# Second token half of a Winograd-form gated feed-forward kernel: transposed on TensorE, or read transposed and scaled in place

## The chip, the cores and the metric

The kernel runs on one core of one Trainium2 chip. The time is the device time of one execution in microseconds (us), told as the median over runs. Five engines take part, each working through its own list of instructions in order: PE (TensorE, matrix products; PEld is its load of stationary operands), DVE (VectorE), ACT (ScalarE), POOL (GpSimd) and SP (SyncE, which here issues nearly all DMAs). An instruction that waits holds back everything behind it on its engine.

## The reference, cut to what matters

```python
x  = L0_attn_data                      # (2, 1024, 512): 2048 tokens, 512 features, float32
xn = (x - mean(x)) / sqrt(var(x) + 1e-5)             # per token
s  = xn @ (weight * block_mask).T                    # 512 -> 512
nx = xn * rsqrt(mean(xn**2) + 1e-5) * ln_w
g  = silu( (silu(nx @ gate_w.T) * (nx @ up_w.T)) @ down_w.T )   # 512 -> 1792 -> 512
out = x + s * g
```

All of it is float32. The kernel normalises a token with a factor `scl` and an offset `nb` (so `xn = x * scl + nb`), both from the token's mean and variance, and feeds the result, transposed so that features lie on partitions, to all products.

## The kernel before, in words

The 2048 tokens are four tiles `t` = 0 to 3 of 512 tokens, and the 512 features four chunks `c` of 128. Every large product is done in Winograd's form on two levels, seven products in place of eight on each. On the outer level the token operand is a 2x2 of blocks B(K, Hh): K is the half of the features, Hh the half of the tokens; so Hh = 1 is tiles 2 and 3. Each block is again a 2x2 of 128x512 pieces (k, n), with c = 2K + k and t = 2Hh + n. The outer products are numbered q: q = 1 and 2 use B(0,0) and B(1,0) as they are, q = 3 uses B(1,1), and q = 5, 6, 7, 4 use sums that `outer_b` forms: S5 = B(0,1) - B(0,0), S6 = B(1,1) - S5, S7 = B(1,1) - B(0,1), S4 = B(1,0) - S6. `inner_b(q, m)` then forms the inner sums m = 5, 6, 7, 4 of each.

The weights come in eight groups `g`: seven of 256 gate and up rows, and the masked linear layer as the last. One outer product of one group is an *instance* j, with seven matmuls of 128x512. The order is all q = 1, 2 of all groups first (instances 0 to 15), then q = 6, 5, 7, 3, 4 of each group, then seven outer products of the down projection.

The schedule is written by hand. `at(pos, fn)` gives every action a position; all are sorted by position and sent to their engines in that order, and no engine reorders. One position is one matmul on PE: `T = lambda us: (us - 14.0) / 0.86` says that position 0 is meant to lie at 14 us and a position to last 0.86 us. Instance j puts its matmuls m = 1, 5, 2, 6, 3, 7, 4 at 7j + 0, 2, 3, 4, 6, 8, 12, so neighbouring instances interleave; they accumulate in PSUM banks `x` (three of them), `y` (two) and `z` (one). Between them, in instances with a sum carried in, DVE takes a snapshot of a bank (`snap`) or adds it up (`total`) and PE continues on that bank only afterwards; in the first instance of each group ACT does it. ACT also copies `x` to `z` as the seed of the `z` product (`seed`, line 350). The product m = 4 of an instance, at 7j + 12, goes into its bank `x` after DVE's `total` of m = 7, which is put at 7j + 9.

Names used below:

- `load_x` (line 121) loads a tile token-major, `stats` (125, 126) and `factors` (139, 140, 137) find `scl` and `nb`, `normalise` (146 on DVE, 148 on ACT) applies them, `transpose` (155) turns 128x128 pieces on PE into a bank `pt` (tag V, two banks), and `evacuate` (163) copies a bank to SBUF. Tiles 0 and 1 go through this before position 8; tiles 2 and 3 between positions 14 and 73, while q = 1, 2 run.
- `add` (97) is the helper for all elementwise sums on DVE and POOL.
- `load_a`, `scale_a` (264, ACT) and `inner_a(g, 1)` (four POOL sums s1, s2, s4, s3 of 128x2x128) prepare the weights of group g for q = 1, 2. The sums are put at positions p - 7, p - 6, p - 5, p - 4, with p = 14g the group's first matmul; the first wants both halves of `scale_a`, which are put at p - 10.4 and p - 7.3.
- `rms_factor`, `rms_store`, `rms_rows` make a second factor per token and hand it out as rows: a transpose of [128, 16] on PE, a copy to SBUF, a DMA to DRAM, and later a DMA that reads a row of DRAM to all 128 partitions.
- `silu` (409, ACT) and `h_out` (414, DVE) form the hidden values, `h_dram` and `acc_dram` take results out (SP).
- `load_final` (565) reads the transposed input `x_t` for the residual at the end.

Of the kernel before, what the change touches and what calls it, by code (L numbers as in the profile page):

```python
# [8 lines left out]
F32 = mybir.dt.float32  # L9
I32 = mybir.dt.int32  # L10
AF = mybir.ActivationFunctionType
ALU = mybir.AluOpType
AX = mybir.AxisListType

P = 128
# [16 lines left out]
def tile_masked_linear_gated_ffn(  # L32
# [21 lines left out]
    rms_dram = tc.dram_tile([NT], F32, name="rms_dram")  # L54
    acc_dram = tc.dram_tile([G + 1, P, 4, W], F32, name="acc_dram")
# [59 lines left out]
    agg = small.tile([P, NTT, TT, 2], F32, tag="agg", name="agg", bufs=1)  # L115
    rms = small.tile([P, NTT, TT], F32, tag="rms", name="rms", bufs=1)
# [11 lines left out]
    def factors(t):  # L128


        scl = small.tile([P, TT], F32, tag="scl", name=f"scl_{t}")
        nb = small.tile([P, TT], F32, tag="nb", name=f"nb_{t}")
        stat[t] = (scl, nb)

        def last():
            nc.vector.reciprocal(scl, scl)
            nc.vector.scalar_tensor_tensor(nb, agg[:, t, :, 0], -1.0, scl, ALU.mult, ALU.mult)

        return [lambda: nc.vector.tensor_scalar(scl, agg[:, t, :, 1], 1.0 + EPS, EPS * EPS, ALU.mult, ALU.add),
                lambda: nc.scalar.activation(scl, scl, AF.Sqrt), last]  # L140
# [36 lines left out]
    def rms_store():  # L177

        b = bank("V", "rms_rows")
        nc.tensor.transpose(b[: NTT * TT, :P], rms.rearrange("p t i -> p (t i)"), ident)  # L180
        rows = small.tile([NTT * TT, P], F32, tag="rms_rows", name="rms_rows", bufs=1)
        nc.vector.tensor_copy(rows, b[: NTT * TT, :P])
        nc.sync.dma_start(rms_dram.rearrange("(i p) -> i p", p=P), rows)
# [7 lines left out]

    bblk, bop = {}, {}

    def outer_b(q, k, n, eng):


        B = lambda K, H_: pt[2 + n, k] if (K, H_) == (0, 1) else raw[2 * K + k, 2 * H_ + n]
        if q in (1, 2, 3):
# [3 lines left out]
        a, b = {  # L202
            5: lambda: (B(0, 1), B(0, 0)),
            6: lambda: (B(1, 1), bblk[5, k, n]),
            7: lambda: (B(1, 1), B(0, 1)),
            4: lambda: (B(1, 0), bblk[6, k, n]),
        }[q]()
        add(eng, o, a, b, ALU.subtract)
# [349 lines left out]
    def load_final(R, Hh, i, slot_s, slot_x):  # L558
# [6 lines left out]
        nc.sync.dma_start(fin[m, t][1], x_t[m * P : (m + 1) * P, t * W : (t + 1) * W])  # L565
# [139 lines left out]
    for t, p, step in ((0, T(7.1), 0), (1, T(12.5), 0), (2, 36.0, 1.2), (3, 36.1, 1.2)):  # L705
        plan(p, step, factors(t))
# [24 lines left out]
    for i in range(TT):  # L731
        at(14.0 + 2.5 * i, stats, 2, i)
        at(25.0 + 3 * i, stats, 3, i)
        at((44.0, 51.0, 55.2, 58.2)[i], normalise, 2, i, act)
        at(40.5 + 2.4 * i, normalise, 3, i, dve)
    plan(36.2, 1.2, rms_factor())

    for t, p0 in ((3, 51.5), (2, 65.5)):
        n = t % 2
        for k, c in enumerate((2, 3, 0, 1)):  # L740
            for i in range(TT):
                at(p0 + 2 * k + 0.01 * i, transpose, t, c, i, "V")
            if c >= 2:
                at(p0 + 2 * k + 1.2, evacuate, t, c, act)
            else:
                at(p0 + 2 * k + 1.2, outer_b, 5, c, n, dve)
                at(p0 + 2 * k + 1.21, outer_b, 7, c, n, dve)
    for k in (0, 1):
        for n in (0, 1):
            at(72, outer_b, 3, k, n, None)  # L750
    for n, p0 in ((1, 60), (0, 74)):
        for k in (0, 1):
            at(p0 + 1.5 * k, outer_b, 6, k, n, dve)
            at(p0 + 2.2 + 1.7 * k + (16 if n == 1 else 4), outer_b, 4, k, n, pool)
    for q, p in ((6, 77), (5, 83), (4, 89), (7, 100), (3, 118)):
# [169 lines left out]
```

## Time and profile before

| what | value |
|---|---|
| runs, us | 513.31, 512.92, 512.67; median 512.92 |
| profiled execution | 513.17 us, its span 511.4 us, granted clock 1.000 |
| busy | PE 505.8 us (99%), DVE 380.4 (74%), POOL 340.9 (67%), ACT 182.6 (36%) |
| busy from 20 to 80 us (of 60) | POOL 15.6 us |
| transposes of `pt` on PE | 64, from 10.1 to 78.3 us |

The span is from the first to the last instruction; the execution's own time has 1.8 us more around it. Busy shares are averages over stages, so they tell which engine is full overall and not what a change in one stage costs. In lines of the trace the columns are start, length, engine, line and operation, the tiles written and read, how many merged instructions, and in brackets how long the engine was idle before and what ended that. A merged piece reaches from its first start to its last end.

### The profile page before, as it was taken

The page shows a single profiled execution, that of the slowest core. Times are in us where ns is not written, and L with a number is a line of the kernel's source. Part 1 is how long each engine was busy: PE and PEld are TensorE (multiplying, and loading weights), DVE is VectorE, ACT ScalarE, POOL GpSimd, SP SyncE. Part 2 cuts the span into 40 slices and gives each one's busy share as a digit, 9 for nine tenths or more (in the row PEclk, how much of TensorE's full clock was granted, in tenths as well). Part 3 has the DMA queues.
Part 4 walks back from the last instruction along what each step waited for, and adds up shares of the span by engine and source line. Part 5 has one row for each costly group of instructions (what it writes and reads, how often), then busy time and mean ns, then how long its engine had stood idle before and what let it go on. Part 6 is the DMA issues. An engine that isn't in the chain of part 4 may idle for free. (4 is left out here: it accounts for less than half of the span.)

```text
span 511.4 us, 4943 instructions
## 1 busy us (share of the span) xinstructions
PE 505.8 (99%) x1269; PEld 231.8 (45%) x1269; DVE 380.4 (74%) x590; ACT 182.6 (36%) x348; POOL 340.9 (67%) x283
## 2 busy tenths in 40 slices
PE   8999999999999999999999999999999999999997
PEld 8444444444444444444444444444444444444444
DVE  6878689876977969699696978968747645367736
ACT  4656754633536353353634433330100101001111
POOL 5522224994795968869597789976662754739960
PEclk9999999999999999999999999999999999999999
DMA  8436636369159386785948667499997698476472
GB/s 289 164 132 238 247 133 227 135 236 350 48 219 348 147 302 228 238 289 208 338 166 294 209 239 254 169 332 383 357 339 270 204 374 327 146 252 216 151 229 83
DMA packets 60460, 121.59 MB, mean 238 GB/s; under 512 B 5760, under 2 KB 13328, under 8 KB 58384
## 3 DMA queue, kind: packets, MB, share of 16 engines
q1 hardware_dynamic: 60288, 121.27, 66.8%
q8 instruction: 10, 0.16, 0.1%
q14 instruction: 18, 0.15, 0.1%
q10 hardware_dynamic: 144, 0.00, 0.0%
HBM read 75.11 MB, written 46.15 MB: 237 GB/s over the span
## 5 line engine op out<-in xcount | busy, mean ns | idle before, releaser
L97 POOL TENSOR_TENSOR mem<-mem 128x512 f32<-128x512 f32 (+4 forms) x245 | 305.2, 1267 | 135.4 <-ACT mem L264 36.5
L343 PE MATMUL x<-mem 128*128 128x512 f32 x448 | 213.6, 595 | 0.2 <-DVE mem L97 0.2
L343 PEld LDWEIGHTS x<-mem 128*128 128x128 f32 x448 | 83.7, 190 | 107.3 <-issue 86.9
L97 DVE TENSOR_TENSOR mem<-x,mem 128x512 f32<-128x512 f32 x137 | 92.5, 684 | 42.0 <-PE x L343 41.1
L343 PE MATMUL y<-mem 128*128 128x512 f32 x224 | 114.5, 593 | 0.3 <-DVE mem L97 0.3
L97 DVE TENSOR_TENSOR mem<-mem 128x512 f32<-128x512 f32 (+3 forms) x60 | 74.7, 1252 | 7.8 <-PE dx L591 4.3
L591 PE MATMUL dx<-mem 128*128 128x512 f32 x174 | 78.3, 592 | 0.0
L97 DVE TENSOR_TENSOR mem<-y,mem 128x512 f32<-128x512 f32 x96 | 65.6, 684 | 9.8 <-PE y L343 8.5
L343 PEld LDWEIGHTS y<-mem 128*128 128x128 f32 x224 | 42.2, 190 | 53.0 <-issue 47.8
L350 ACT COPY z<-x 128x512 f32<-128x512 f32 x54 | 30.9, 573 | 97.9 <-PE x L343 92.2
L343 PE MATMUL z<-mem 128*128 128x512 f32 x112 | 57.3, 593 | 0.0
L591 PEld LDWEIGHTS dx<-mem 128*128 128x128 f32 x174 | 33.1, 190 | 41.6 <-issue 40.4
L591 PE MATMUL dy<-mem 128*128 128x512 f32 x98 | 44.5, 592 | 0.0
L409 ACT ACTIVATE gate<-mem 128x512 f32<-128x512 f32 x56 | 33.1, 601 | 25.3 <-DVE mem L97 20.9
L414 DVE TENSOR_TENSOR mem<-gate,mem 128x512 f32<-128x512 f32 x56 | 38.0, 681 | 5.1 <-POOL mem L97 4.3
L564 POOL TENSOR_TENSOR mem<-mem 128x512 f32<-128x512 f32 x16 | 25.0, 1570 | 15.3 <-DMA mem<-s_dram 15.2
L343 PEld LDWEIGHTS z<-mem 128*128 128x128 f32 x112 | 21.0, 190 | 24.9 <-issue 23.9
L574 ACT ACTIVATE silu<-mem 128x512 f32<-128x512 f32 x15 | 9.0, 602 | 64.6 <-DVE mem L97 48.3
L97 DVE TENSOR_TENSOR mem<-z,mem 128x512 f32<-128x512 f32 x41 | 28.0, 682 | 3.5 <-PE z L343 3.5
L591 PEld LDWEIGHTS dy<-mem 128*128 128x128 f32 x98 | 18.6, 190 | 23.4 <-issue 23.4
L97 DVE TENSOR_TENSOR mem<-dx,mem 128x512 f32<-128x512 f32 x16 | 11.0, 690 | 20.1 <-PE dx L591 20.1
L591 PE MATMUL dz<-mem 128*128 128x512 f32 x56 | 25.2, 592 | 0.0
(73 smaller groups left out, 289.2 us busy)
## 6 DMA issues: line engine op xcount, KB each, us to landing
h_dram<-mem SPq DMA_DIRECT2D x98, 256.0 KB, 2.1
mem<-h_dram SPq DMA_DIRECT2D x28, 768.0 KB, 6.2
mem<-in_gu SPq DMA_DIRECT2D x42, 256.0 KB, 3.7
acc_dram<-mem SPq DMA_DIRECT2D x8, 1024.0 KB, 4.2
mem<-acc_dram SPq DMA_DIRECT2D x8, 1024.0 KB, 6.7
mem<-in_x SPq DMA_DIRECT2D x16, 256.0 KB, 5.2
s_dram<-mem SPq DMA_DIRECT2D x16, 256.0 KB, 4.8
mem<-s_dram SPq DMA_DIRECT2D x16, 256.0 KB, 6.3
```

The costliest lines, as they stand in the source:

```text
L97: eng.tensor_tensor(o, a, b, op)
L343: nc.tensor.matmul(st[key], weights(g, q, m), operand(q, m), start=first and not (key == "z" and seeded), stop=True, skip_group_check=True)
L350: nc.scalar.copy(st["z"], st["x"])
L409: nc.scalar.activation(gate[key], t(), AF.Silu)
L414: nc.vector.tensor_mul(a(), gate[key], b())
L564: at_later.append(lambda: nc.gpsimd.tensor_tensor(s_tile, s_tile, rms_bc[t], ALU.mult))
L574: nc.scalar.activation(b[0][:, part], y[:, part] if source is None else source(), AF.Silu)
L591: nc.tensor.matmul(st[key], w(), b(), start=first and key != "z", stop=True, skip_group_check=True)
```

## The change

Tiles 2 and 3 are no longer normalised token-major and transposed on PE. Their transposed form is read from DRAM (`x_t`, now laid out so that each 128x512 piece is one block), and the factor and the offset, which then vary along the free dimension, are handed out as rows: `fac_rows(t)` transposes the [128, 8] of `scl` and `nb` on PE, ACT copies the result, SP writes it to DRAM and reads each of the two rows back to all partitions. `scale_xt(t, c, f)` on POOL multiplies a piece by the factor row (f = 0) or adds the offset row (f = 1), in place. The offset row is added to B(1,1) alone: the sums are rearranged so that B(0,1) is needed only in S7 = B(1,1) - B(0,1), where the offset drops out, and then S6 = S7 + B(0,0), S5 = B(1,1) - S6, S4 = B(1,0) - S6.

The 32 transposes, 4 evacuations and 8 normalisations of these two tiles go. Eight loads of pieces, two transposes and copies, two stores and four row reads come. Twelve scalings and, for n = 1, the sums S7 and S6 are put on POOL. In each half n the order of positions is p0 + 0, 1.5, 3, 4.5 for the four multiplications (c = 0, 2, 1, 3), then S7, then p0 + 9, 10.5 for the offsets (c = 2, 3), then S6, S5, S4; p0 is 31 for n = 1 and 50 for n = 0. Statistics of tile 3 now come before those of tile 2, at positions 14 to 21.5 and 23.5 to 31.9; the factors at 22.6 to 23.8 (tile 3) and 33.4 to 35.8 (tile 2); `fac_rows` at 24.5 and 40.8; the inner sums of q = 6, 5, 4, 7 start at 68, 75, 81, 96 in place of 77, 83, 89, 100.

```diff
+    fac_dram = tc.dram_tile([2, 2, W], F32, name="fac_dram")
...
+    fac = small.tile([P, 2, 2, TT], F32, tag="fac", name="fac", bufs=1)
...
     def factors(t):
-        scl = small.tile([P, TT], F32, tag="scl", name=f"scl_{t}")
-        nb = small.tile([P, TT], F32, tag="nb", name=f"nb_{t}")
+        if t < 2:
+            scl = small.tile([P, TT], F32, tag="scl", name=f"scl_{t}")
+            nb = small.tile([P, TT], F32, tag="nb", name=f"nb_{t}")
+        else:
+            scl, nb = fac[:, t - 2, 0, :], fac[:, t - 2, 1, :]
...
+    def load_xt(t, c):
+        K, k, n = c // 2, c % 2, t % 2
+        v = mem[:, F["v5"] + 4 + 2 * n + k, :] if K == 0 else slot("tmp" if (k, n) == (0, 1) else "B3")
+        (u12 if K == 0 else raw)[(k, n) if K == 0 else (c, t)] = v
+        nc.sync.dma_start(v, x_t[c, t])
+
+    def fac_rows(t):
+        b = bank("V", f"fac_rows_{t}")
+        nc.tensor.transpose(b[: 2 * TT, :P], fac[:, t - 2].rearrange("p f i -> p (f i)"), ident)
+        rows = small.tile([2 * TT, P], F32, tag="rows", name=f"fac_sb_{t}")
+        nc.scalar.copy(rows, b[: 2 * TT, :P])
+        nc.sync.dma_start(fac_dram[t - 2].rearrange("f (i p) -> (f i) p", p=P), rows)
+        for f in range(2):
+            fac_bc[t, f] = mem[:, F["B6"] + 3 + 2 * (t - 2) + f, :]
+            nc.sync.dma_start(fac_bc[t, f], fac_dram[t - 2, f].unsqueeze(0).to_broadcast([P, W]))
+
+    def scale_xt(t, c, f):
+        v = u12[c, t % 2] if c < 2 else raw[c, t]
+        add(pool, v, v, fac_bc[t, f], (ALU.mult, ALU.add)[f])
...
-            5: lambda: (B(0, 1), B(0, 0)),
-            6: lambda: (B(1, 1), bblk[5, k, n]),
-            7: lambda: (B(1, 1), B(0, 1)),
-            4: lambda: (B(1, 0), bblk[6, k, n]),
+            7: lambda: (B(1, 1), u12[k, n], ALU.subtract),
+            6: lambda: (bblk[7, k, n], B(0, 0), ALU.add),
+            5: lambda: (B(1, 1), bblk[6, k, n], ALU.subtract),
+            4: lambda: (B(1, 0), bblk[6, k, n], ALU.subtract),
...
-    for t, p, step in ((0, T(7.1), 0), (1, T(12.5), 0), (2, 36.0, 1.2), (3, 36.1, 1.2)):
+    for t, p, step in ((0, T(7.1), 0), (1, T(12.5), 0), (3, 22.6, 0.6), (2, 33.4, 1.2)):
         plan(p, step, factors(t))
...
-        at(14.0 + 2.5 * i, stats, 2, i)
-        at(25.0 + 3 * i, stats, 3, i)
-        at((44.0, 51.0, 55.2, 58.2)[i], normalise, 2, i, act)
-        at(40.5 + 2.4 * i, normalise, 3, i, dve)
-    plan(36.2, 1.2, rms_factor())
-    for t, p0 in ((3, 51.5), (2, 65.5)):
-        n = t % 2
-        for k, c in enumerate((2, 3, 0, 1)):
-            for i in range(TT):
-                at(p0 + 2 * k + 0.01 * i, transpose, t, c, i, "V")
-            if c >= 2:
-                at(p0 + 2 * k + 1.2, evacuate, t, c, act)
-            else:
-                at(p0 + 2 * k + 1.2, outer_b, 5, c, n, dve)
-                at(p0 + 2 * k + 1.21, outer_b, 7, c, n, dve)
+        at(14.0 + 2.5 * i, stats, 3, i)
+        at(23.5 + 2.8 * i, stats, 2, i)
+    plan(37.5, 1.2, rms_factor())
+    for k, (t, c) in enumerate((t, c) for t in (3, 2) for c in (0, 2, 1, 3)):
+        at(21.0 + 1.5 * k, load_xt, t, c)
+    at(24.5, fac_rows, 3)
+    at(40.8, fac_rows, 2)
+    for n, p0 in ((1, 31), (0, 50)):
+        t = 2 + n
+        for off, c, f in ((0, 0, 0), (1.5, 2, 0), (3, 1, 0), (4.5, 3, 0), (9, 2, 1), (10.5, 3, 1)):
+            at(p0 + off, scale_xt, t, c, f)
+        for off, q, k, eng in (((6, 7, 0, pool), (7.5, 7, 1, pool), (12, 6, 0, pool), (13.5, 6, 1, pool), (13.7, 5, 0, dve), (15.5, 5, 1, dve),
+                                (16, 4, 0, pool), (17.3, 4, 1, pool)) if n else
+                               ((6, 7, 0, dve), (8, 7, 1, dve), (11, 6, 0, dve), (12.5, 6, 1, dve), (14.7, 5, 0, dve), (16.7, 5, 1, dve),
+                                (15, 4, 0, pool), (16.5, 4, 1, pool))):
+            at(p0 + off, outer_b, q, k, n, eng)
...
-    for n, p0 in ((1, 60), (0, 74)):
-        for k in (0, 1):
-            at(p0 + 1.5 * k, outer_b, 6, k, n, dve)
-            at(p0 + 2.2 + 1.7 * k + (16 if n == 1 else 4), outer_b, 4, k, n, pool)
-    for q, p in ((6, 77), (5, 83), (4, 89), (7, 100), (3, 118)):
+    for q, p in ((6, 68), (5, 75), (4, 81), (7, 96), (3, 118)):
         for off, m, eng in ((0, 5, dve), (3, 6, dve), (5.5, 7, pool), (7.5, 4, pool)):
             at(p + off, inner_b, q, m, eng)
...
-        "x_t": x.reshape(B * S, H).T,
+        "x_t": x.reshape(-1, W, KC, P).transpose(2, 0, 3, 1),
```

## The prediction, made before the changed kernel ran

> **What bounds the kernel now.** I read the page's busy table first, then PE's instructions and waits, then the timelines of the four engines from 20 to 110 us.
>
> ```profile
> PE 505.8 (99%) x1269; PEld 231.8 (45%) x1269; DVE 380.4 (74%) x590; ACT 182.6 (36%) x348; POOL 340.9 (67%) x283
> ...
> PE y L343 <- DVE mem L97: 0.3, 1, 0.3
> ```
>
> The second line is nearly all that PE waits for after 20 us. PE has no slack: what leaves it shortens the run, and what makes it wait lengthens it. PE's timeline prices the transposes:
>
> ```profile
> 59.90 0.60 PE L155 MATMUL pt<-ident,mem 128*128 128x128 f32 x4
> 60.34 1.02 PE L343 MATMUL x<-mem 128*128 128x512 f32 x2
> ...
> 64.21 0.60 PE L155 MATMUL pt<-ident,mem 128*128 128x128 f32 x4
> 64.65 1.02 PE L343 MATMUL y<-mem 128*128 128x512 f32 x2
> 65.51 1.02 PE L343 MATMUL z<-mem 128*128 128x512 f32 x2
> 66.37 1.88 PE L343 MATMUL x<-mem 128*128 128x512 f32 x4
> ```
>
> A set of four takes 0.435 us from its start to the next one's, a matmul position 0.86. The last line's second half, at 67.23, is position 61: instance 7's m = 4. I use it as the milestone. POOL looks idle here, but where it works its pieces are long:
>
> ```profile
> 44.10 3.05 POOL L97 TENSOR_TENSOR mem<-mem 128x256 f32<-128x256 f32 x4 [9.46 <-ACT mem L264]
> ...
> 144.85 5.08 POOL L97 TENSOR_TENSOR mem<-mem 128x512 f32<-128x512 f32 x4
> ```
>
> So 0.76 us for a weight sum and 1.27 for a 128x512 sum. ACT's timeline gives the chain around the weight scaling, and the group of the one existing row transpose the DMA trip:
>
> ```profile
> 41.64 0.58 ACT L361 COPY mem<-x 128x512 f32<-128x512 f32 x1 [0.33 <-PE x L343]
> 42.12 0.59 ACT L371 COPY mem<-z 128x512 f32<-128x512 f32 x1
> 42.59 0.62 ACT L409 ACTIVATE gate<-mem 128x512 f32<-128x512 f32 x1
> 43.13 0.90 ACT L264 ACTIVATE mem<-mem,lnw_sb 128x256 f32<-128x256 f32 x2
> 44.27 0.57 ACT L350 COPY z<-x 128x512 f32<-128x512 f32 x1 [0.24 <-PE x L343]
> 44.85 1.28 ACT L140 ACT_TABLE_LOAD   x1
> ...
> DMA to landing us min/median/max: 4.0/4.0/4.0
> ```
>
> **What the Trainium skill says.** "SBUF — State Buffer", section "SBUF: two separate sides": the port pair that DVE and GpSimd share is "an exclusive lock, not a bandwidth split", also for a DVE operation with two SBUF inputs. The trace agrees that they collide, with a price for each side: a DVE sum of two SBUF tiles takes 0.67 us alone and 1.18 beside POOL, and four POOL sums at 89.93 us took 5.91 in place of 5.08.
>
> ```profile
> 85.80 1.18 DVE L97 TENSOR_TENSOR mem<-mem 128x512 f32<-128x512 f32 x1
> 88.70 0.67 DVE L97 TENSOR_TENSOR mem<-mem 128x512 f32<-128x512 f32 x1
> ```
>
> "ScalarE: Activation LUTs", section "What ACT_TABLE_LOAD costs", gives about 1283 ns for a load, whatever the set; the trace has 1.28 us. What that page adds for a drain behind it I don't use: here work follows 1.3 us after the load's start.
>
> **The change part by part.**
>
> *PE work.* Minus 8 sets x 0.435 = -3.48 us; plus two row transposes at a quarter of a set, +0.22. Together -3.26.
>
> *DVE and ACT work removed* (8 normalisations at 0.54 or 0.80, 4 evacuations at 0.58, four DVE sums at 0.68 net): no direct gain, PE didn't wait for them.
>
> *Row transpose of tile 3, position 24.5.* PE would reach it at 34.57, after the z product that starts at 33.71. DVE ends tile 3's last statistics where it ended tile 2's before, at 32.91. Behind it come the factor (0.24), a total (0.6), tile 2's first statistics (0.9), reciprocal and offset (0.2 each): 34.9. With PE's weight loads for the row (0.09) and the next product (0.19) uncovered, the next product starts at about 35.25, or 0.65 late (0.4 to 0.9). Behind it everything on PE waits. ACT holds its gate table load until it has copied the row, to 35.75; its gates end near 38.1, and the next z seed, due at 38.85 with the delay, still fits.
>
> *Table load of tile 2's factor.* The load and square root (1.3 + 0.2) now sit ahead of `scale_a` and the z seed of instance 5. From 42.3 (41.64 plus the delay): 0.48 + 0.47 + 0.6 + 1.5 + 0.9, so `scale_a` ends at 46.3 where it ended at 44.0, and the seed at 46.8. The z product at 45.73, now due at 46.4, starts near 47: +0.6 (0.3 to 0.8). With the second row transpose PE is 1.3 us behind a run without transposes. That row's own factors are ready about 3 us before PE.
>
> *Row trip of tile 3.* Row in SBUF at 35.75, store issued at 36. SP then stands on the landing, and two piece loads and two h_dram stores queue behind it; nobody needs those before POOL's fourth scaling. The store lands in 2.0 (the page's h_dram stores) to 4.0 us (the rms row, in a busier stretch); the read in 2.9 (weights in this stretch) to 6.1 (rms rows, busy). I take the short ends, as the DMA engines idle here: 41.2. Three scalings of 1.27 end at 45.0, ahead of `scale_a`, so a landing up to 42.4 costs nothing. The long ends give 46.4, 4 us more. Tile 2's row is ready 5 us before POOL gets to it. The eight piece loads (2 MB) lie in stretches where the DMA engines are half idle: nothing.
>
> *POOL.* This is the main term. From `scale_a`'s end at 46.3 POOL has, in its order: s1, scaling, s2, S7, s4, s3, S7, two offsets, S6; that is six of 1.27 and four of 0.76 = 10.7, so S6 (n = 1) ends at 57.0. DVE wants it at 52.9, for S5, and stands: a wait that the kernel didn't have. Behind S5 are a gate product, the second S5, two totals, a gate product, and the total for which PE's position 54 waits, due at 60.7. Seven at 0.6 plus a collision end at 61.3 to 62.0: about 1.3 us on PE. POOL goes on with the second S6, two S4, s1, scaling, s2, s4, scaling, s3 and two scalings, seven of 1.27 and four of 0.76 = 11.9: 68.9, or 69.8 with two collisions of 0.45. Only then can DVE form S7 (k = 1, n = 0), and behind that stands the total of instance 7's m = 7, for which the milestone waits. S7 0.6 to 1.0, total 0.69, 0.25 to PE: 70.5 to 71.5, middle 71.0, in place of 67.23. This takes in all delays above; they don't add to it. POOL's weight sums themselves stay over 2 us ahead of PE.
>
> *After the milestone.* PE and DVE start level. To instance 9's snapshot, which PE needs ten positions on (8.6 us), DVE has 15 operations at 0.6 = 9.0, five of them two-SBUF sums that may lose 0.3 to 0.5: a further 0.4 to 2.4; I take 0.7. From position 75 on the inner sums come earlier than before and 35 positions ahead of need: nothing.
>
> *Sum.* Milestone 71.0 - 67.23 = +3.8. The before kernel still has four sets of transposes behind it: -1.74. Backlog +0.7. Net **+2.7** on the profiled execution's 513.17: 515.9. The median run is 0.25 lower, so I say **515.6 us**.
>
> **Rivals.**
>
> 1. *POOL's lag is absorbed* (the other side). DVE's totals lie three positions ahead of PE's need, and POOL was idle for 44 of the 60 us from 20 to 80. If S6 and S7 come in time, only the row transpose and the z seed remain: -3.26 + 0.65 - 0.11 + 0.6 = -2.1, **510.8 us**. Against it: POOL's order holds 10.7 us of work where DVE's need leaves 6.6. It decides from S7's last scaling ending before about 65 us.
> 2. *The row comes late.* At the long ends, 46.4 in place of 42.4, POOL's chain and all behind it move by up to 4 us: **518 to 519.6**. For it: SP issues everything in order and the only row store in the trace took 4.0. Against: that was in a busy stretch.
> 3. *Near balance.* No collisions, no backlog, short waits: milestone 70.3, +3.1 - 1.74 = +1.3, or down to +0.5 if DVE's first stand is shorter: about **513.6**.
> 4. *The change doesn't do what it says*, for instance PE keeps its transposes: the instruction lists show them gone, so I leave it without a chance.
>
> **How the numbers follow.** Forecast 0.58, rival 1 0.17, rival 2 0.14, rival 3 0.11. Differences under 0.2%, about 1 us, can't be told from none: rival 3 is that case, so faster 0.17, same 0.11, slower 0.72. The likeliest case's own range is 514.2 (no collision) to 517.4 (backlog of 2.4). To hold 8 in 10 the range takes in rival 3, half of rival 2 and the nearer part of rival 1: 511.4 to 518.5.
>
> **What would show it.** In the changed profile: PE's idle before `x` released by DVE should grow from nothing to 4 to 6 us in 34 to 82 us, with DVE's idle released by POOL `mem L97` at about 53 and again near 67; POOL full from 46 to 72; a piece of 0.5 us on the z product near 46. If POOL's scalings start after 43, rival 2 holds. If PE shows under 1.5 us of idle there, the POOL term is wrong and the kernel is faster. If POOL sums of this shape take near 1.05 us in place of 1.27, the chain is 2 us shorter and the result lies near no change.

## The result, and the profile after

| | before | after |
|---|---|---|
| median of 4 runs each | 513.05 us (512.67 to 513.31) | 518.84 us (518.57 to 519.59) |
| profiled execution, its span | 513.17, 511.4 us | 519.59, 517.8 us |
| granted clock of the profiled execution | 1.000 | 0.993 |

The ratio is 1.0116, 95% interval 1.0098 to 1.0133: slower by 5.8 us, where 2.7 were predicted. The profiled execution is the slowest of the four. First the page, its busy line and the clock in 40 slices of 12.9 us:

```profile
PE 505.6 (98%) x1239; PEld 229.0 (44%) x1239; DVE 385.4 (74%) x582; ACT 178.0 (34%) x342; POOL 362.1 (70%) x299
...
PEclk9999979999999999999999999999999999999999
```

PE has 30 instructions less than before, yet is busy for the same time: the sixth digit of the clock, a 7 for 70%, says why. What PE waited for between 20 and 130 us (total, times, longest):

```profile
PE x L372 <- DVE mem L98: 5.9, 1, 5.9
PE y L372 <- DVE mem L98: 0.3, 1, 0.3
PE fac_rows L208 <- DVE fac L142: 0.3, 1, 0.3
PE z L372 <- ACT z L379: 0.2, 1, 0.2
```

It is one standstill. PE's timeline around it:

```profile
59.53 1.02 PE L372 MATMUL x<-mem 128*128 128x512 f32 x2
66.42 2.07 PE L372 MATMUL x<-mem 128*128 128x512 f32 x2 [5.87 <-DVE mem L98]
68.29 1.91 PE L372 MATMUL y<-mem 128*128 128x512 f32 x2
70.00 2.61 PE L372 MATMUL x<-mem 128*128 128x512 f32 x4
72.45 1.02 PE L372 MATMUL y<-mem 128*128 128x512 f32 x2
```

And one row of the table by windows (width, busy time of PE, PEld, DVE, ACT, POOL, then granted clock, DMA share, GB/s):

```profile
66.00:72.00 6.00, 5.58 (x7) 2.36 (x8) 4.14 (x7) 0.80 (x2) 3.89 (x4) 0.54 1.00 346
```

The product at 66.42 is position 54. A matmul of 128x512 appears as two instructions, 1.02 us for the pair; behind the standstill pairs take 2.07 and 1.91, and the clock in that window is 0.54. The prediction had PE 1.3 us late here, and no lower clock. The milestone, position 61, starts at 75.02 instead of 67.23 (predicted 71.0). DVE's timeline shows who is late:

```profile
52.01 0.69 DVE L98 TENSOR_TENSOR mem<-x,mem 128x512 f32<-128x512 f32 x1 [0.95 <-PE x L372]
56.01 6.77 DVE L98 TENSOR_TENSOR mem<-mem 128x512 f32<-128x512 f32 x1 [3.30 <-POOL mem L98]
62.70 0.68 DVE L443 TENSOR_TENSOR mem<-gate,mem 128x512 f32<-128x512 f32 x1
```

The second line is S5 of n = 1. DVE stood 3.30 us for S6, where the prediction had 4.1, and then the sum itself took 6.77 us. POOL's timeline has the long chain that the prediction counted out, 21 operations (sums and scalings) from 45.83 to 68.24:

```profile
40.13 3.73 POOL L98 TENSOR_TENSOR mem<-mem 128x512 f32<-128x512 f32 x3 [5.80 <-DMA mem<-fac_dram]
45.83 22.41 POOL L98 TENSOR_TENSOR mem<-mem 128x256 f32<-128x256 f32 x21 [1.97 <-ACT mem L293]
```

While S5 stood, POOL did six operations; S5 ended 0.55 us after POOL's first stop, of 0.08 us at 62.23 ahead of a sum that needs its own predecessor.

The difference of product starts between the two traces gives the account. After the first 10 us: +0.53 at the first row transpose, +0.34 at the z seed of instance 5, +0.26 at the second row transpose, +6.03 at the standstill, +2.6 by the slow clock, -3.5 for the eight sets of transposes: +6.3, less 0.3 us of an earlier start. From position 72 to the end nothing more is lost: +6.04 us there, +6.06 at 484 us.

### The profile page after: what moved, and what is told of

The parts are those of the page before. It is cut to its first block, busy times and chain, and to the rows that moved or that the text cites. A ratio compares the mean times of both kernels' runs of the same rounds, so it can differ in the third digit from the quotient of the medians.

```text
span 517.8 us, 4901 instructions
## 1 busy us (share of the span) xinstructions
PE 505.6 (98%) x1239; PEld 229.0 (44%) x1239; DVE 385.4 (74%) x582; ACT 178.0 (34%) x342; POOL 362.1 (70%) x299
## 5 line engine op out<-in xcount | busy, mean ns | idle before, releaser
L98 POOL TENSOR_TENSOR mem<-mem 128x512 f32<-128x512 f32 (+4 forms) x261 | 326.2, 1273 | 121.1 <-ACT mem L400 32.3
L98 DVE TENSOR_TENSOR mem<-x,mem 128x512 f32<-128x512 f32 x137 | 92.4, 683 | 43.5 <-PE x L372 42.5
L98 DVE TENSOR_TENSOR mem<-mem 128x512 f32<-128x512 f32 (+2 forms) x64 | 85.0, 1332 | 10.3 <-PE dx L620 4.4
```

Source lines behind the costliest of these rows:

```text
L98: eng.tensor_tensor(o, a, b, op)
```

## The experiments

17 further kernels ran, three of them with added phases whose own time means nothing. In the table, every offset is the start of a product on PE in the kernel's trace minus its start in the kernel before; medians are beside 513.0 to 513.4 for the kernel before, run alongside. The offsets hold a difference from the start-up, already there at 20 us, of -0.3 us (changed, e8_other_sums, e13_inner_back) to +0.7 (e3_gap). "S5" is the length of the first S5 of n = 1. Positions and S5 are from one profiled execution of each kernel. f1 and f2 are single runs.

| kernel | position 54 | position 61 | position 72 | S5, us | median, us | ratio (95%) |
|---|---|---|---|---|---|---|
| changed | +6.09 | +7.80 | +6.04 | 6.77 | 518.84 | 1.0116 (1.0098, 1.0133) |
| e1_filler | +6.29 | +5.51 | +3.76 | 6.77 | 517.04 | 1.0072 (1.0057, 1.0087) |
| e2_s5_late | +0.06 | +3.05 | +4.31 | moved | 517.63 | 1.0083 (1.0066, 1.01) |
| e3_gap | +2.87 | +5.31 | +5.93 | 0.69 | 518.97 | 1.011 (1.0095, 1.0125) |
| e9_stop | +1.81 | +4.25 | +5.53 | 1.74 | 518.60 | 1.0104 (1.0081, 1.0127) |
| e10_stop_filler | +2.51 | +7.74 | +5.99 | 1.74 | 519.22 | 1.0113 (1.0096, 1.013) |
| e12_stop_filler3 | +2.32 | +4.75 | +5.57 | 1.74 | 518.56 | 1.0101 (1.0085, 1.0118) |
| e13_inner_back | +1.70 | +4.13 | +3.87 | 1.74 | 517.40 | 1.0088 (1.0073, 1.0103) |
| e14_only_inner_back | +2.03 | +4.46 | +4.51 | 1.74 | 517.81 | 1.0088 (1.0071, 1.0105) |
| e8_other_sums | +1.54 | +3.97 | +6.31 | 1.74 | 520.08 | 1.0122 (1.0097, 1.0147) |
| f1_first_s4 | +2.12 | +3.34 | +4.55 | 1.74 | 518.17 | |
| f2_second_s4 | +1.94 | +3.14 | +2.23 | 1.75 | 515.78 | |
| e6_s4_late | +1.27 | +1.81 | +1.89 | 1.75 | 515.42 | 1.0041 (1.0028, 1.0054) |
| e5_rearranged | +1.17 | +0.29 | -1.47 | moved | 514.41 | 1.0023 (1.0014, 1.0031) |
| e7_best | +0.59 | -0.29 | -2.05 | moved | 511.62 | 0.9972 (0.9962, 0.9983) |

From position 61 to 72 a kernel without pt transposes gains 1.74 on the kernel before; what it gains less is a slow clock or waits in between.

### Is the slow stretch the clock's doing?

**e1_filler** keeps PE busy through the standstill with seven products of a zero tile.

```diff
+        if j == 7:
+            for _ in range(7):
+                at(7 * j + 4.5, lambda: nc.tensor.matmul(st["x"], zero, operand(1, 1), start=False, stop=True,
+                                                         skip_group_check=True))
```

> The changed kernel with seven extra matmuls of 128x512 on PE just ahead of position 54. Their stationary operand is all zeros and they add to instance 7's bank x, so the sums stay as they are. They take 7 x 0.86 = 6.0 us, about the 5.9 us for which PE stood there. Theory (the standstill lowered TensorE's granted clock, and the matmuls of 66.4 to 72.4 us ran at half speed for that reason, 2.6 us): position 54 starts at about 66.5 as before, its records take 0.59 us and not 1.0, and the run takes 516.2 us (515.8 to 516.7). Rival (they were slow for their operands or for what ran beside them): 518.8 us as in the changed kernel, records still near 1 us.

Its PE timeline, the filler first:

```profile
60.59 6.17 PE L409 MATMUL x<-mem,zero 128*128 128x512 f32 x14
66.63 1.12 PE L375 MATMUL x<-mem 128*128 128x512 f32 x2
67.59 1.02 PE L375 MATMUL y<-mem 128*128 128x512 f32 x2
```

Position 54 starts no earlier, but the products behind it take 1.12 and 1.02 instead of 2.07 and 1.91. The median fell by 1.8 us of the 2.6 that the slow records add up to, and so ended 0.3 us above the range expected; between the two profiled executions the difference is 2.5. So here the clock falls because PE stood, and adding work makes this kernel faster.

### S5 moved, or POOL's order changed

**e2_s5_late** puts S5 of n = 1 on DVE at positions 72 and 73.5.

```diff
-  (13.7, 5, 0, dve), (15.5, 5, 1, dve),
+  (41, 5, 0, dve), (42.5, 5, 1, dve),
```

> The changed kernel with the two sums S5 of n = 1 moved on DVE from positions 44.7 and 46.5 to 72 and 73.5; nothing else. Theory (S5, a DVE sum of two SBUF tiles, found no way in while POOL's instructions followed each other without a gap, 56.0 to 62.8 us): PE's 5.9 us and the slow clock behind them go, 8.6 us together. In their place S7 (n = 0) now stands until POOL's run ends near 68.3, and PE waits at position 61 until about 71 where it would come at 66.4. Time 518.8 - 8.6 + 4.7 = 514.9 us (513.5 to 516.5). Rival (DVE was simply too far behind, and S5 was only where it showed): 518 to 519 us, with PE's standstill still at position 54.

**e3_gap** lets S4 (k = 0) follow S6 (k = 0) at once, so that POOL has to stop between them.

```diff
-  (12, 6, 0, pool), (13.5, 6, 1, pool), (13.7, 5, 0, dve), (15.5, 5, 1, dve), (16, 4, 0, pool), (17.3, 4, 1, pool)
+  (12, 6, 0, pool), (12.1, 4, 0, pool), (13.5, 6, 1, pool), (13.7, 5, 0, dve), (15.5, 5, 1, dve), (17.3, 4, 1, pool)
```

> The changed kernel with one swap in POOL's order: S4 (k = 0, n = 1) goes straight behind S6 (k = 0), on which it depends, and S6 (k = 1) comes after it. POOL must then end S6 before S4 may start, a gap of some 0.08 us, in the very place where DVE's S5 becomes ready. Theory (DVE gets in at POOL's first gap): S5 lasts 0.7 to 1.3 us in place of 6.8, PE stands 1 to 3 us at position 54 and again before position 61, and the run takes about 515.2 us (513.5 to 516.5). Rival (S5 waited for its data, or for POOL to have nothing left to do): S5 lasts 6 us or more and the time is 518.5 to 520 us.

In both the 6.77 us are gone, and in both PE stands later instead. One line of PE's timeline of each, position 61:

```profile
70.27 2.08 PE L372 MATMUL x<-mem 128*128 128x512 f32 x2 [3.71 <-DVE mem L98]
```

```profile
72.54 1.12 PE L372 MATMUL x<-mem 128*128 128x512 f32 x2 [3.06 <-DVE mem L98]
```

The times missed what I expected by 2.7 and 3.8 us: 517.63 and 518.97. Position 61 is the milestone, and the wait is the one that the prediction put there: DVE can form S7 (k = 1, n = 0) only when POOL has done its last scalings. In e2_s5_late the low clock follows at once (0.65 from 72 to 78 us); in the profiled execution of e3_gap it doesn't.

### The shut-out taken away, and nothing else

**e9_stop** puts a copy of 128x4 behind S6 (k = 1) on POOL that reads S6's result.

```diff
+    stop = small.tile([P, 4], F32, tag="stop", name="stop", bufs=1)
+    at(31 + 15.9, lambda: nc.gpsimd.tensor_copy(stop, bblk[6, 1, 1][:, :4]))
```

> The changed kernel with one 128x4 copy put into POOL's queue behind S6(k=1) that reads what S6(k=1) wrote, so that POOL has to stop for an instant (as ahead of s4, 0.08 us) before it, and then goes on with S4 as before; nothing else is changed. Theory (S5 gets in at the first stop of POOL): S5 lasts 1.75 us instead of 6.8, position 54 starts near 61.5 at full clock, and the time falls to about 513.5 to 515.5, though a POOL instruction was added. Rival (the stop has nothing to do with it): S5 lasts 6.8 us, or at least 3, and the time stays at 518 to 520.

S5 and the S7 ahead of position 61 on DVE's timeline:

```profile
56.14 1.74 DVE L98 TENSOR_TENSOR mem<-mem 128x512 f32<-128x512 f32 x1 [3.31 <-POOL mem L98]
...
69.09 1.74 DVE L98 TENSOR_TENSOR mem<-mem 128x512 f32<-128x512 f32 x1 [1.79 <-POOL mem L98]
```

And four lines of PE's:

```profile
62.15 1.13 PE L372 MATMUL x<-mem 128*128 128x512 f32 x2 [1.47 <-DVE mem L98]
71.48 2.08 PE L372 MATMUL x<-mem 128*128 128x512 f32 x2 [3.06 <-DVE mem L98]
73.35 1.91 PE L372 MATMUL y<-mem 128*128 128x512 f32 x2
75.06 3.06 PE L372 MATMUL x<-mem 128*128 128x512 f32 x4
```

S5 takes 1.74 us, position 54 comes 4.3 us earlier, and the time is 518.6: what I expected of S5 came true and what I expected of the time didn't. This trace is the prediction's forecast almost to the letter: 1.47 us of wait at position 54 (predicted 1.3), position 61 at 71.48 (71.0). But behind it stand pairs of 1.91 us again: from +4.25 at position 61 the offset grows to +7.29 four products later. The low clock takes 3.0 us. Its row by windows:

```profile
72.00:78.00 6.00, 6.00 (x9) 2.26 (x8) 5.62 (x8) 0.57 (x1) 5.92 (x7) 0.55 0.43 135
```

Cut finer, the granted clock is 0.50 from 70.58 to 77.41 us here and from 64.64 to 71.46 in the changed kernel, and 1.00 around that. PE works through 5.9 and 5.0 us of these 6.83, and half of that is about the 3.0 and 2.6 us lost. The four executions of e9_stop differ in this: 519.09 (the profiled one) and 519.80 us have a mean clock of 0.993, 517.91 and 518.12 have 1.000 and 0.996. The median lies between the two pairs.

### And the slow clock taken away too

**e10_stop_filler** is e9_stop with seven zero products ahead of position 61; **e12_stop_filler3** has `range(3)` in the same place.

```diff
+        if j == 8:
+            for _ in range(7):
+                at(7 * j + 4.5, lambda: nc.tensor.matmul(st["x"], zero, operand(1, 1), start=False, stop=True,
+                                                         skip_group_check=True))
```

> The run e9_stop (S5 let in at once, 1.74 us; PE stands 3.06 us ahead of position 61, which starts at 71.48, and is granted a low clock for some 8 us behind it) with seven matmuls of a zero weight tile, which add nothing, put into bank x ahead of position 61, so that PE is busy while it waits for S7. Theory (what the prediction's sum lacks is the clock that a standstill of about 3 us costs): position 61 starts at 71.5 as in e9_stop, all products behind it are at full clock, 3.0 us of the delay go (position 61 is 4.25 us later than before and the products behind it up to 7.29), and the time is 515.2 to 516.2, about what was predicted. Rival (the slow records are a matter of what waits behind the standstill, not of PE's idling): position 61 and the time stay, 518.0 to 519.

> The run e10_stop_filler with 3 zero-weight matmuls ahead of position 61 instead of 7. Each of them takes 0.86 us there, so that the seven kept PE for 6.0 us, twice as long as the standstill of 3.06 us that they should fill; three take 2.6. Theory (the prediction's sum lacks the clock that a standstill of about 3 us costs): the products up to position 61 keep their times of e9_stop, position 61 starts at 71.5 to 72.3 (PE gets to it with what is left of the wait), everything behind it is at full clock, and the time is 515.2 to 516.5. Rival (clock and standstill don't belong together): slow records behind position 61 as in e9_stop, 518 to 519.

e10_stop_filler says nothing on the time (519.22, where 515.2 to 516.2 were expected): I had counted the two instructions of a product as two products, and 6.0 us of filler stood in a gap of 3.06. It shows only that the clock stays at 1.00. With three, from PE's timeline:

```profile
68.77 2.74 PE L409 MATMUL x<-mem,zero 128*128 128x512 f32 x6
71.97 1.12 PE L375 MATMUL x<-mem 128*128 128x512 f32 x2 [0.47 <-DVE mem L99]
...
80.46 1.02 PE L375 MATMUL x<-mem 128*128 128x512 f32 x2
83.03 1.13 PE L375 MATMUL x<-mem 128*128 128x512 f32 x2 [1.55 <-DVE mem L99]
```

The clock is 1.00 throughout, position 61 comes at 71.97, and the time is 518.56 once more, where 515.2 to 516.5 were expected. Now PE waits at 83.03 (position 71): after the milestone 2.56 us are lost (+4.75 - 1.74 = +3.01, measured +5.57). DVE's timeline shows it behind with sums that collide with POOL:

```profile
76.41 1.24 DVE L99 TENSOR_TENSOR mem<-mem 128x512 f32<-128x512 f32 x1
79.37 1.33 DVE L99 TENSOR_TENSOR mem<-mem 128x512 f32<-128x512 f32 x1
```

These take 0.67 alone. That is the prediction's backlog, put at 0.7 us with 2.4 as its upper end. In e9_stop and in the changed kernel nothing is lost between the end of the slow clock and position 72; my reading is that the slow clock holds PE back while DVE catches up. It doesn't always cover it: in e8_other_sums, which has two more sums on POOL in that stretch, 1.8 us of slow clock (+3.97 to +5.77) and 2.3 us of waits (+6.31 instead of +4.03) were both paid.

### The backlog

**e13_inner_back** is e12_stop_filler3 with the inner sums of B where they were before; **e14_only_inner_back** is the changed kernel with that alone.

```diff
-    for q, p in ((6, 68), (5, 75), (4, 81), (7, 96), (3, 118)):
+    for q, p in ((6, 77), (5, 83), (4, 89), (7, 100), (3, 118)):
```

> The run e12_stop_filler3 with the inner sums of B put back to the positions of the kernel before (q = 6, 5, 4, 7 at 77, 83, 89, 100 instead of 68, 75, 81, 96). In e12_stop_filler3 the clock stays full and position 61 starts at 71.97, near the predicted 71.0, but DVE is then full from 72 to 82 us, five of its sums of two SBUF tiles take 1.15 to 1.33 beside POOL, and position 69 waits for it at 83.03: 2.5 us after the milestone where the prediction had 0.7. Theory (that backlog is made by the earlier inner sums, which the prediction priced at nothing): two DVE sums and two POOL sums leave the stretch from 72 to 82, the waits behind the milestone fall from 2.5 to under 0.8, and the time is 516.2 to 517.2. Rival (the backlog is what DVE owes after its stands for S6 and S7, wherever the inner sums are): it stays over 1.8, 518 to 519.

> The changed kernel with only this part undone: the inner sums of B at the positions of the kernel before. There the standstill and the slow clock give DVE the time that the inner sums take, and nothing is lost behind position 61. Theory (limits of about the same length stand behind one another, and one that is hidden costs nothing): 518.3 to 519.4, no change. Rival (the earlier inner sums cost what they cost in e12_stop_filler3): 516.5 to 517.5.

(Position 69 in that text is the product that starts at 83.03, position 71.) That product in e13_inner_back:

```profile
81.33 1.13 PE L375 MATMUL x<-mem 128*128 128x512 f32 x2 [0.47 <-DVE mem L99]
```

In e13_inner_back the backlog fell from 2.56 to 1.48 us (+4.13 - 1.74 = +2.39, measured +3.87), between what the two expected, and the time to 517.40. Three DVE sums of 0.86, 1.25 and 1.33 in place of 0.67 make 1.43: what is left fits collisions. So the earlier inner sums, priced at nothing, cost 1.1 us once nothing else covers them.

e14_only_inner_back isn't the clean test that I meant it to be: its median is 1.0 us below the changed kernel's (the intervals of the ratios overlap), but S5 took 1.74 there, and PE stood 3.04 us at position 61 and lost 1.8 to a low clock, 3.41 us of 0.50.

```profile
56.50 1.74 DVE L98 TENSOR_TENSOR mem<-mem 128x512 f32<-128x512 f32 x1 [3.29 <-POOL mem L98]
```

```profile
71.69 1.60 PE L372 MATMUL x<-mem 128*128 128x512 f32 x2 [3.04 <-DVE mem L98]
```

### Why S5 stood so long

Phases added behind the last product of the kernel before measure the collision by itself: POOL adds tiles back to back, and a DVE sum of two SBUF tiles waits for one of them. **e4_micro** varies DVE's operands and what POOL does behind, **m2_micro** takes the very tiles and order behind S6, **m3_micro** varies how long POOL ran before.

> The kernel before with five short phases added behind its end, on SBUF tiles that nobody uses any more. In each, POOL forms one 128x512 sum, DVE starts one instruction that reads it, and POOL goes on with n more sums: (1) n = 6 that don't depend on each other, DVE a sum of two SBUF tiles; (2) the same with each POOL sum reading the one before it; (3) as 1 with n = 12; (4) as 1, but DVE's second input in PSUM; (5) as 1, but DVE a multiply-add of one SBUF tile with two constants. Theory (shut out until POOL's first gap): DVE's instruction lasts about 7.5 us, 0.7 to 1.3, about 15, 0.7, and in phase 5 either 0.5 or about 7.5. Rival (it loses at most the one POOL instruction that runs): at most 2 us in every phase. The whole time is that of the kernel before plus 50 to 70 us.

> The kernel before with six phases behind its end. Each has POOL form one 128x512 sum that a DVE difference of two SBUF tiles reads, and POOL goes on without that difference. (1) The very tiles, forms and order of POOL's instructions behind S6 in the changed kernel, where S5 lasted 6.8 us: three 128x512 sums, a weight sum s1, a scaling, s2, and s4 that must wait for s2. (2) DVE's tiles the same, POOL's instructions six plain 128x512 sums. (3) As 1, but POOL's two S4 no longer read what S6 wrote. (4) As 1 up to the third sum, then plain sums. (5) POOL as 1, DVE on other tiles for its result and first input. (6) Plain sums in place of the first three, then s1, scaling, s2, s4. Theory (POOL instructions that follow without a wait for their forerunner keep DVE out, given something in this order that the first set of phases lacked): phase 1 gives 6 to 7 us, phase 2 at most 1.8, and the others tell what it is: the reads of a fresh sum (3 short), the weight sums (4 short, 6 long), DVE's own tiles (5 short). Rival (it needs what else runs in that place: PE, ACT or DMAs): every phase at most 1.8 us.

> The kernel before with six added phases behind its last product, so its own time means nothing; what is read is the duration of one DVE sum in each phase. In a phase ScalarE copies one tile, POOL adds 1, 3, 5, 8, 10 or 10 independent 128x512 tiles back to back, a DVE sum with both operands in SBUF waits for the last of them, and POOL goes on with 6 more independent sums. In the sixth phase the ninth of the ten reads the eighth, so that POOL stops for an instant there. Theory (after a long run of POOL without an instant's stop DVE isn't let in until POOL next stops): at most 1.8 us for 1 and 3, about 6 x 1.07 + 0.3 = 6.7 us for 8 and 10, at most 1.8 again in the sixth phase. Rival (the length of POOL's run has nothing to do with it, DVE loses one POOL instruction at most): at most 1.8 us in all six.

All three theories failed and the rivals held: DVE lost one POOL sum at most. Its instruction took 1.73 or 1.74 us in phases 1 and 3 of e4_micro and in all six of m2_micro and of m3_micro, 1.47 with one SBUF operand, 0.69 where POOL's sums were chained or DVE read one operand from PSUM. From m3_micro, the phase with ten sums ahead, DVE's sum:

```profile
578.83 1.74 DVE L97 TENSOR_TENSOR mem<-mem 128x512 f32<-128x512 f32 x1 [13.00 <-POOL mem L97]
```

and POOL's run of sixteen around it:

```profile
566.56 20.01 POOL L97 TENSOR_TENSOR mem<-mem 128x512 f32<-128x512 f32 x16 [1.46 <-ACT mem L881]
```

In the kernel itself, **e8_other_sums** moves both S4 of n = 1 sixteen positions on and puts two other sums in their places; **f1_first_s4** moves only the second S4 (16 and 33 in the first lines of the diff), **f2_second_s4** only the first (32 and 17.3).

```diff
-  (16, 4, 0, pool), (17.3, 4, 1, pool)
+  (32, 4, 0, pool), (33, 4, 1, pool)
...
+    for i in range(2):
+        at(31 + 16 + 1.3 * i, lambda i=i: add(pool, spare(i), raw[2, 3], raw[3, 3]))
```

> The run e6_s4_late (S4 of n=1 16 positions later on POOL) with two other 128x512 sums on POOL in the places that S4 left; they add two raw tiles into the slots that S4 will write later, so their result is overwritten and they do nothing but keep POOL going behind S6. Theory (S5 gets in at the first instant at which POOL stops; in e6_s4_late that was 1.20 us in, at 57.41, ahead of s1): with two sums that wait for nothing POOL goes on without a stop to s4 as in the changed kernel, S5 lasts 6.8 us again, and the time is about that of the changed kernel plus the two later S4: 518 to 520. Rival (it is S4 itself, its operands or its slots, that shut S5 out): S5 lasts at most 1.8 us and the time stays within 1.5 us of 515.4.

> The changed kernel with only the second of the two S4 of n=1 moved 16 positions later on POOL: behind S6(k=1) POOL has S4(k=0), s1, a scaling, s2 and the stop ahead of s4. One look, for the length of S5. If it is S4(k=0) at the first boundary that keeps DVE out until POOL stops, S5 ends 0.55 us after that stop begins, about 5.5 us long; if it is S4(k=1), or both together, S5 takes 1.75.

> The changed kernel with only the first of the two S4 of n=1 moved 16 positions later on POOL: behind S6(k=1) POOL has S4(k=1), s1, a scaling, s2. One look, for the length of S5. If it is S4(k=0) that keeps DVE out, S5 takes 1.75 us; if it is S4(k=1), about 5.5; if any sum of this kind behind S6 does, 5.5 in both of these runs.

S5 took 1.74 or 1.75 in all three, also where POOL went on without a stop. (e8_other_sums took about the time expected, 520.08, but not for that reason.) And in e14_only_inner_back, whose lists on all engines are those of the changed kernel until more than 15 us behind S5, it took 1.74. So POOL's run, its stops, the operands and the order don't by themselves decide the 6.77 us, seen in the profiled executions of the changed kernel and e1_filler. Nor does the moment at which S5 starts: POOL's sum had begun 0.073 and 0.089 us before it in these two, and 0.065 to 0.092 us before it in the nine profiled executions with 1.74 or 1.75. What decides it stays open.

### POOL's chain made shorter, and the waits designed out

**e6_s4_late** moves both S4 of n = 1 off the chain that S7 waits for.

```diff
-  (16, 4, 0, pool), (17.3, 4, 1, pool)
+  (32, 4, 0, pool), (33, 4, 1, pool)
```

> The changed kernel with S4 of n=1 (two POOL sums behind S6) moved 16 positions later on POOL. Behind S6(k=1), which starts as S5 is let loose near 56.0, POOL then has s1, a scaling and s2, and its next stop (s4 waits for s2) comes two instructions of 1.23 us earlier. Theory (DVE is shut out until POOL next stops): S5 ends near 60.3 instead of 62.8, about 4.3 instead of 6.8 us long, position 54 starts near 64.0, and the time falls by 2.5 us and by what the shorter standstill spares of the slow clock (up to 2 us more): 514.5 to 516.4 us. Rival 1 (the operands of S4 or an accident of that moment shut DVE out): S5 lasts at most 2 us, position 54 starts by 62, about 513. Rival 2 (S5's length is fixed by something that isn't POOL's): still 6.8 us and 518.8 us.

Position 61 on PE:

```profile
69.04 1.13 PE L372 MATMUL x<-mem 128*128 128x512 f32 x2 [1.16 <-ACT mem L400]
```

(ACT's copy and DVE's total behind S7 end at the same moment there, 68.99.) Taking two sums of 1.23 us out of the chain brought 3.4 us against the changed kernel and 3.2 against e9_stop, where S5 is as short: S7 ends at 68.4, 2.4 earlier than in e9_stop, PE no longer stands 3 us, and the clock stays at 1.00. That the time fell into the range expected was luck: the reason for it (S5 held until a stop, 4.3 us) was wrong, S5 took 1.75.

**e5_rearranged** leaves the chain on POOL and moves what DVE needs of it behind its end; **e7_best** also mends what PE still waited for there. The diff is e7_best's. Besides, both put the offsets of n = 0 at 50 + 15 and 16 and `fac_rows(2)` later (42.3 in e7_best, 43.5 in e5_rearranged), and the q = 3 blocks, which cost no instruction, at 76 in place of 73. e5_rearranged has the inner sum m = 6 of q = 6 still on DVE, `fac_rows(3)` at 27.5 in place of 24.5, the factors of tile 2 from 36.3 on and `rms_factor` from 38.5 on.

```diff
-(13.7, 5, 0, dve), (15.5, 5, 1, dve), (16, 4, 0, pool), (17.3, 4, 1, pool)) if n else
-((6, 7, 0, dve), (8, 7, 1, dve), (11, 6, 0, dve), (12.5, 6, 1, dve), (14.7, 5, 0, dve), (16.7, 5, 1, dve),
- (15, 4, 0, pool), (16.5, 4, 1, pool))
+(16, 4, 0, pool), (17.3, 4, 1, pool), (40, 5, 0, dve), (41.5, 5, 1, dve)) if n else
+((13, 7, 0, dve), (14.5, 7, 1, dve), (17, 6, 0, dve), (18.5, 6, 1, dve), (23, 5, 0, dve), (24.5, 5, 1, dve),
+ (24, 4, 0, pool), (25, 4, 1, pool))
...
-for q, p in ((6, 68), (5, 75), (4, 81), (7, 96), (3, 118)):
-    for off, m, eng in ((0, 5, dve), (3, 6, dve), (5.5, 7, pool), (7.5, 4, pool)):
+for q, p in ((6, 77), (5, 83), (4, 89), (7, 100), (3, 118)):
+    for off, m, eng in ((0, 5, dve), (3, 6, pool if q == 6 else dve), (5.5, 7, pool), (7.5, 4, pool)):
```

> The changed kernel with the same instructions in another order. S7, S6, S5 of n = 0 go to positions 63, 64.5, 67, 68.5, 73, 74.5 and the offsets of tile 2 to 65 and 66; S5 of n = 1 to 71 and 72.5; the inner sums of q = 6, 5, 4, 7 back to 77, 83, 89, 100; the factor of tile 2 behind the z seed of instance 5 (36.3) and the row transposes to 27.5 and 43.5. DVE then reaches each sum when POOL has done what it needs. Theory (the changed kernel lost its time to DVE standing for POOL, 6.0 us with S5's long one, to the slow clock behind that, 2.6, and to two short waits, 0.9): all of it goes, only the 3.3 us saved on PE remain, and the run takes 510.0 us (509.6 to 511.5). Rival (POOL has no room for 16 more operations in this stage wherever they are put, or DVE is shut out at another place): 513 us or more, with PE's standstill before another total.

> The order of the run e5_rearranged, with what PE waited for there undone: row transposes at 24.5 and 42.3 and the factors of tile 2 at the changed kernel's places and pace (in e5_rearranged the first transpose waited 0.94 us and position 41 waited 0.67), and the second inner sum of q=6 on POOL instead of DVE (position 81 waited 0.57 behind a full DVE). If these waits are what kept e5_rearranged from its gain, PE gains 1 to 2 us on it: 512.2 to 513.6 us, against 513.3 for the kernel before. Rival (the spread of its runs, 513.4 to 515.3, comes from collisions of DVE with the 20 added POOL sums, which stay): 514 to 514.5 us again.

(Positions 41 and 81 in that text count the products; they are 43 and 83 in the schedule.) e5_rearranged missed its 510.0 by 4.4 us: the standstills were gone, but the first row transpose alone cost PE 1.16 us. Its profiled execution, 513.40, is the fastest of thirteen, so the trace shows only a part of what the median lost. e7_best is 1.6 us faster than the kernel before and 7.2 faster than the changed one; it beat the range expected by 0.6 us. What PE waits for from 20 to 130 us:

```profile
PE y L372 <- DVE mem L98: 0.3, 1, 0.3
PE fac_rows L208 <- DVE fac L142: 0.3, 1, 0.3
PE z L372 <- ACT z L379: 0.2, 1, 0.2
```

And POOL's timeline, with the chain as long as ever:

```profile
46.24 21.62 POOL L98 TENSOR_TENSOR mem<-mem 128x256 f32<-128x256 f32 x21 [1.18 <-ACT mem L293]
```

DVE's waits for POOL, 3.3 us in the changed kernel from 50 to 75 us, are absent there.

## Why the prediction was right or wrong

The side was right: slower, by POOL's lag. The size was 3 us short, and two terms of the sum failed. The first is S5 "plus a collision", with PE 1.3 us late at position 54: PE stood 5.87 us there. The second is what follows the wait, which the sum put at +0.7 for DVE's backlog and at nothing for the clock. Without the first failure (e9_stop) the low clock alone takes 3.0 us; with the clock kept as well (e12_stop_filler3) the backlog takes 2.56. Point by point:

- **PE work, -3.26 us.** Right: -3.5 for the sets, +0.26 for the second row transpose.
- **Row transpose of tile 3, +0.65; z seed, +0.6.** 0.53 and 0.34; both inside their bounds.
- **Row trip at the short ends, 41.2.** The first scaling starts at 40.13, before the 42.4 from which a delay would cost. Rival 2 is out, though the time lies in its range of 518 to 519.6.
- **POOL's chain.** `scale_a` ends at 45.8 (46.3), S6 at 55.97 (57.0): POOL's 128x512 sums follow each other every 1.23 us, not every 1.27, and the ten operations took 10.1 us in place of 10.7. DVE's stand of 3.30 us had been put at 4.1. Rival 1 is out: nothing absorbed it.
- **S5 "plus a collision", PE about 1.3 us late at position 54.** This step failed in the changed kernel: S5 took 6.77 us instead of about 1.2, and PE stood 5.87 us. A plain collision had been priced low too: 0.5 us more than the 0.67 alone, where a sum that comes as POOL begins one took 1.74, 1.07 more. The Trainium skill, "SBUF — State Buffer", section "SBUF: two separate sides", has the loser blocked for one whole instruction of the other; the collisions of 1.74 us agree with that, this one lasted for six and goes beyond the page. The sign "4 to 6 us of idle on PE" came true in its number by coincidence: as one wait at position 54, not as a small one there and a larger one at 61.
- **A term that the sum doesn't hold: the clock.** The Trainium skill, "TensorE: Matmul & The Clock Gate", section "HAM oscillation — how this bites in real kernels", gives the rule of no PE idle gaps above about 3.4 us. The trace of before, with no wait over 0.3 us after the start, could not show it. Here a stand of 5.87 us cost 2.6 us of slow clock and one of 3.71 (e2_s5_late) 3.0. After 3.04 to 3.06 us of recorded idle it cost 1.8 to 3.0 in e8_other_sums, e9_stop and e14_only_inner_back, but nothing in the profiled execution of e3_gap (one of its other three has a mean clock of 0.993). So a recorded gap somewhat below the page's figure can be enough, and not every gap of that length counts; since the ends of products are modelled in these records, the limit isn't measured closer. Having forecast 4 to 6 us of idle on PE, the prediction should have priced this.
- **Milestone at 71.0.** 75.02 in the changed kernel; 71.48 and 71.97 in e9_stop and e12_stop_filler3, where S5 wasn't shut out. The second started 0.5 us later. This step held as soon as the accident was gone. (The upper end of its sum is 71.7, not 71.5.)
- **Backlog, +0.7 (0.4 to 2.4).** Nothing shows in the changed kernel, where the slow clock seems to cover it; 2.56 where nothing covers it (e12_stop_filler3), 1.1 of that from the inner sums that were priced at nothing. The sum's upper end was near, the 0.7 taken from it was not.

So removing the 6.77 us instruction that stands out in the profile doesn't shorten the run. Taken away, it gives 518.60; with the clock kept as well, 518.56. Behind S5's shut-out stood the wait for S7, behind that wait's slow clock stood DVE's backlog, all of nearly the same length. In hindsight the sum should have taken, on top of the milestone's +3.8 and the -1.74, the larger of the clock's 3.0 and the backlog's 2.5: about +5, near the +5.5 of e9_stop and e12_stop_filler3. What is shown to shorten the run most is a shorter chain on POOL ahead of DVE's need (e6_s4_late), or DVE not needing it (e7_best).

Not tried: pieces of S7 or S6 on DVE, and a second profile of the changed kernel to see how often S5 is shut out; its four runs lie within 1.0 us.

## What to carry to other kernels

Price a wait on the bottleneck engine with what follows it: a PE standstill of 3.0 us or more brought 1.8 to 3.0 us of slow clock on top in five of the six profiled executions that had one, and there can be debts of the helper engines that this slowness hides. When the largest stall of a profile is removed and the time stays, look at the next wait in the same chain before doubting the reading: the remedy is to shorten the chain, or to move its consumers behind its end. Work moved "at no cost" into a stretch that is about to become late has a cost there.

## What the runs showed of the hardware that was not expected

- A DVE sum of two 128x512 SBUF tiles beside back-to-back POOL sums lost at most about one POOL sum everywhere else (up to 1.80 us), but twice lost six operations (6.768 and 6.774 us) with the same instructions around it as in e14_only_inner_back; it then ended 0.55 us after POOL's first stop of 0.08 us.
- The price has two sides: where DVE gets in between two POOL sums, POOL's next 128x512 sum takes 1.71 to 1.78 us instead of 1.27.
- Small DVE operations suffer too: three of 16 elements per partition took 0.69, 0.90 and 0.65 us in the changed kernel, each ending 0.03 us after the POOL operation that ran beside it. In the kernel before, the first and the last began between two POOL operations and took 0.16 and 0.17; the middle one took 0.34 and also ended 0.03 us after POOL's.
- The slow clock came in stretches of two lengths: 0.50 for 6.83 us in the changed kernel, e2_s5_late and e9_stop, and for 3.41 us in e8_other_sums and e14_only_inner_back. In the last two it began 0.5 us after PE had gone on.
- Seven products of a zero tile, 6 us of added PE work, made the changed kernel 1.8 us faster, because they kept the clock up.
